# Attention by even and odd heads on partition halves, and a feed-forward in token groups of 512 with output chunks of 128, in a block of windowed attention and Fourier layer

## Chip, cores, metric

One core of a Trainium2 chip. The metric is the device time of one launch in microseconds (us). Most runs of one kernel lie within 0.3% of its median. A ratio compares the fast runs of one kernel with the fast runs of the kernel before in the same rounds, as the record gives it, with a 95% interval. It is not quite the ratio of the medians that stand beside it.

## The reference, cut to what matters

32 images of 56 by 56 tokens and 128 channels, all in fp32.

```python
# layer 0: windows of 7x7 (49 tokens), shifted by 3, 4 heads of 32 channels
q, k, v = split(win @ w_qkv.T)                      # per window and head: 49 x 32
attn = softmax(scale * q @ k.T + bias + mask)       # 49 x 49
x = x + unwindow((attn @ v) @ w_proj.T + b_proj)    # groupnorm of x ahead of it
# layer 1: along rows and along columns: DCT, 32 modes, a 128x128 mix per mode, inverse DCT
h = fourier_rows(gn(x), w0) + fourier_cols(gn(x), w1)
x = x + relu(h @ W1 + b1) @ W2 + b2                 # 128 -> 512 -> 128, 3136 tokens an image
```

## The kernel before

A "row" is one row of eight windows; an image has eight, so there are 256. Each engine works through its own queue of instructions in the order of the built program. The build may shift independent pieces against each other. An edit of the source's order therefore sets the built order only indirectly. Attention of one image is issued row by row; the Fourier layer and feed-forward of the image before (`conv_layer`) is a generator. Each of its pieces ends with a `yield` of its estimated TensorE time, and the main loop lets it run a share ahead of the next row's scores and a share ahead of this row's output:

```python
    for R, (b, i) in enumerate(rows):
        im = images[b]
        share = PE_CONV / NWR / 2 if R >= NWR + LAG else 0.0
        # ... loading and norm of the next image (cut)
        advance(share)                       # run conv_layer pieces for `share` us
        if R + 1 < len(rows):
            attn_scores(images[rows[R + 1][0]], rows[R + 1][1])
        advance(share)
        attn_out(im, i)
```

The weighted values: four transposes of the softmax (TensorE), a copy out of PSUM, the memory that TensorE writes, into `aT` (VectorE; such a copy is called an evacuation below), then the product with a `v` whose second half holds zeros, so that the result comes out per pair of heads:

```python
            for m in range(4):
                nc.tensor.transpose(pt[:, m * P : (m + 1) * P], a[:, hp, pr]..., ident)   # cut
            aT = work.tile([P, 4, 2, JP], F32, tag="aT", name="aT")
            nc.vector.tensor_copy(aT.rearrange("p m a j -> p (m a j)"), pt)
            ...
                        nc.tensor.matmul(
                            po3[hp * JP : (hp + 1) * JP, :, x0 : x0 + s1 - s0],
                            lhsT=v[:, w, hp].rearrange("j h d -> j (h d)"),
                            rhs=aT[:, 2 * (w4 // 2) + hp, w % 2, 0:WT]...,              # cut
                            start=True, stop=True)
```

The inverse transform of rows and the feed-forward. `back` makes two transposes (TensorE), one copy into `zT` (ScalarE) and eight products (TensorE); `rows_back` then adds the result to `xf` (VectorE):

```python
        rows_back(0)
        yield 0.65
        for g in range(NG):                  # 7 groups of 448 tokens
            ...
            for f in range(NF):              # first product (FF1): 4 x 448 columns
                nc.tensor.matmul(ph[:, :GT], lhsT=wff1[:, f * P : (f + 1) * P], rhs=xf[group g], ...)
                nc.scalar.activation(hf, ph[:, :GT], AF.Relu, bias=b1sb[:, f : f + 1])
            yield 3.0
            if g + 1 < NG:
                rows_back(g + 1)             # one group ahead, BETWEEN the two products
                yield 0.65
            for c in range(4):               # second product (FF2): 4 chunks of 112 tokens
                for f in range(NF):
                    nc.tensor.matmul(pf[:TC, ...], lhsT=hid[f][:, c * TC : (c + 1) * TC], rhs=wff2[:, f], ...)
            ...
            yield 3.5
```

Of the kernel before, what the change touches and what calls it, by code (L numbers as in the profile page):

```python
# [15 lines left out]
P = 128  # L16
S = 56
# [24 lines left out]
HIDBUFS = 5  # L42
LAG = 1
# [4 lines left out]
def swin_fourier_kernel(  # L48
# [104 lines left out]
    mask_sb = const_load([P, 2, 3, WT], shift_mask.rearrange("r s p j -> p r s j"), "mask")  # L153
    bm = const.tile([P, 2, 2, NWR // 2, 2, WT], F32, tag="bm", name="bm")
    rpb_f = rpb.rearrange("p (t h) y x -> p t h (y x)", t=2)
    for r in range(2):
        for pr in range(NWR // 2):
            for t in range(2):
                nc.vector.tensor_tensor(
                    bm[:, r, t, pr],  # L160
                    rpb_f[:, t],
                    mask_sb[:, r, 0 if pr < NWR // 2 - 1 else 2]
                    .unsqueeze(1)
                    .to_broadcast([P, 2, WT]),
                    ALU.add,
                )
# [21 lines left out]
    b2sb = const_load([TC, C], b2.partition_broadcast(TC), "b2sb")  # L188
# [9 lines left out]
    q_sb, v_bd, a_sb = [], [], []  # L198
    for i in range(2):
        q_sb.append(big.tile([P, RT + JP - WT], F32, tag=f"q{i}", name=f"q{i}"))  # L200
        v_bd.append(big.tile([P, NWR, 2, 2, HD], F32, tag=f"v{i}", name=f"v{i}"))
        a_sb.append(big.tile([P, 2, NWR // 2, 2, JP], F32, tag=f"a{i}", name=f"a{i}"))
        nc.gpsimd.memset(q_sb[i], 0.0)
        nc.gpsimd.memset(v_bd[i], 0.0)
        nc.gpsimd.memset(a_sb[i], 0.0)
# [7 lines left out]
    def image_begin(b):  # L213
        im = Image()
        im.b = b
        im.x = xls.pop(b) if b in xls else load_image(b)
        im.xw = big.tile([P, NWR, RT], F32, tag="xw", name="xw", bufs=2)
        im.st = small.tile([P, NWR, 6], F32, tag="st0", name="st0", bufs=2)
        im.part = small.tile([TC, 2, C // 4, NWR], F32, tag="part", name="part", bufs=2)
        im.scr = dram.tile([S, S, C], F32, tag="scr", name="scr", bufs=2)  # L220
        return im

    def image_group(im, i):



        pt = attn_bank()
        pt4 = pt[:, : 8 * S].rearrange("p (j r s) -> p j r s", r=8, s=WS)
        for c in range(4):
            nc.tensor.transpose(  # L230
                pt4[:, :, 2 * c : 2 * c + 2],
                im.x[:, WS * i // 2 + c],
                ident_x[:, :, SS:].rearrange("p r (j s) -> p j r s", s=WS),
            )
        mine = pt4[:, :, i % 2 : i % 2 + WS].rearrange("p j r s -> p j (r s)")
        xw = im.xw[:, i]
        nc.scalar.copy(xw.rearrange("p (j t) -> p j t", t=WT), mine)
        nc.vector.bn_stats(im.st[:, i], xw)

        n0, n1 = WS * i // 2, WS * (i + 1) // 2  # L240
        piece = im.x[:, n0:n1]
        nc.gpsimd.tensor_tensor(  # L242
            piece, piece, bproj.unsqueeze(1).to_broadcast([TC, n1 - n0, C]), ALU.add
        )
# [36 lines left out]
    def attn_scores(im, i):  # L281

        q, v, a = q_sb[i % 2], v_bd[i % 2], a_sb[i % 2]
        src = im.xw[:, i]
# [16 lines left out]
        wv = im.w[:, 2 * C : 3 * C].rearrange("c (p h d) -> c h p d", h=2, d=HD)  # L301
        for w in range(NWR):
            for hh in range(2):
                nc.tensor.matmul(  # L304
                    pv[hh * JP : hh * JP + WT, w * JP : (w + 1) * JP],
                    lhsT=src[:, w * WT : (w + 1) * WT],
                    rhs=wv[:, hh],
                    start=True,
                    stop=True,
                )  # L310
        for hh in range(2):
            rows = slice(hh * JP, hh * JP + WT)
            nc.scalar.copy(  # L313
                v[rows, :, :, hh].rearrange("j w p d -> j (w p) d"),
                pv[rows].rearrange("j (x d) -> j x d", d=HD),
            )


        ps = [attn_bank(), attn_bank()]
        for w in range(NWR):  # L320
            for hp in range(2):
                cs = slice(hp * JP, (hp + 1) * JP)
                qs = slice((w % 2) * JP, (w % 2 + 1) * JP)
                nc.tensor.matmul(  # L324
                    ps[hp][qs, (w // 2) * 2 * WT : (w // 2 + 1) * 2 * WT],
                    lhsT=q[cs, w * WT : w * WT + JP],
                    rhs=k_bd[cs, w].rearrange("c h j -> c (h j)"),
                    start=True,
                    stop=True,
                )  # L330
        NR = NWR // 2 * 2
# [3 lines left out]
        for hp in range(2):  # L335
            a3 = a[:, hp].rearrange("p a h j -> p (a h) j")[:, :, 0:WT]
            nc.vector.tensor_tensor(  # L337
                a3,
                ps[hp][:, :RT].rearrange("p (m j) -> p m j", j=WT),
                bm[:, i // (NWR - 1), hp].rearrange("p a h j -> p (a h) j"),  # L340
                ALU.add,
            )
        a3 = a.rearrange("p t a h j -> p (t a h) j")[:, :, 0:WT]
# [12 lines left out]
    def attn_out(im, i):  # L356

        v, a = v_bd[i % 2], a_sb[i % 2]
        po = attn_bank()
        po3 = po[:, :RT].rearrange("p (r x) -> p r x", x=S)  # L360
        for hf in range(2):
            pt = attn_bank()
            for m in range(4):
                pr, hp = 2 * hf + m // 2, m % 2
                nc.tensor.transpose(  # L365
                    pt[:, m * P : (m + 1) * P],
                    a[:, hp, pr].rearrange("p h j -> p (h j)"),
                    ident,
                )
            aT = work.tile([P, 4, 2, JP], F32, tag="aT", name="aT")  # L370
            nc.vector.tensor_copy(aT.rearrange("p m a j -> p (m a j)"), pt)  # L371
            for w4 in range(4):
                w = 4 * hf + w4

                x0 = w * WS + SS
                cuts = ((0, WS, x0),) if w < NWR - 1 else ((0, WS - SS, x0), (WS - SS, WS, 0))
                for s0, s1, x0 in cuts:
                    for hp in range(2):
                        nc.tensor.matmul(  # L379
                            po3[hp * JP : (hp + 1) * JP, :, x0 : x0 + s1 - s0],  # L380
                            lhsT=v[:, w, hp].rearrange("j h d -> j (h d)"),
                            rhs=aT[:, 2 * (w4 // 2) + hp, w % 2, 0:WT].rearrange(
                                "j (r s) -> j r s", s=WS
                            )[:, :, s0:s1],
                            start=True,
                            stop=True,
                        )

        if i % 2 == 0:
            im.oT = work.tile([P, 2 * RT], F32, tag="oT", name="oT")  # L390
        oT = im.oT
        nc.scalar.activation(
            oT[:, i % 2 * RT : (i % 2 + 1) * RT], po[:, :RT], AF.Identity, bias=im.bias[:, 2:3]
        )
# [35 lines left out]
    def conv_layer(im):  # L430
# [158 lines left out]
        rows_back(0)  # L589
        yield 0.65  # L590
        for g in range(NG):
            res = work.tile([TC, 4, C], F32, tag="res", name="res")
            nc.sync.dma_start(
                res, im.scr[8 * g : 8 * g + 8].rearrange("(n r) w c -> (r w) n c", r=2)
            )
            nc.gpsimd.tensor_tensor(  # L596
                res, res, b2sb.unsqueeze(1).to_broadcast([TC, 4, C]), ALU.add
            )
            hid = []
            for f in range(NF):  # L600
                ph = conv_bank()
                nc.tensor.matmul(  # L602
                    ph[:, :GT],
                    lhsT=wff1[:, f * P : (f + 1) * P],
                    rhs=xf[:, 8 * g : 8 * g + 8].rearrange("p r w -> p (r w)"),
# [3 lines left out]
                hf = work.tile([P, GT], F32, tag="hid", name="hid", bufs=HIDBUFS)  # L609
                nc.scalar.activation(hf, ph[:, :GT], AF.Relu, bias=b1sb[:, f : f + 1])  # L610
                hid.append(hf)
            yield 3.0
            if g + 1 < NG:
                rows_back(g + 1)
                yield 0.65
            pf = conv_bank()
            for c in range(4):
                for f in range(NF):
                    nc.tensor.matmul(  # L619
                        pf[:TC, c * C : (c + 1) * C],  # L620
                        lhsT=hid[f][:, c * TC : (c + 1) * TC],
                        rhs=wff2[:, f],
                        start=(f == 0),
                        stop=(f == NF - 1),
                    )
            nc.vector.tensor_tensor(
                res, pf[:TC].rearrange("p (n c) -> p n c", c=C), res, ALU.add
            )
            for n0, n1, p, dst in chunks_of(out, b, 4 * g, 4 * g + 4):
                nc.sync.dma_start(dst, res[p, n0 - 4 * g : n1 - 4 * g])  # L630
            yield 3.5
# [106 lines left out]
```

## Time and profile before

| | before |
|---|---|
| median of the first three runs | 4977.4 us (4976.43 to 4993.0) |
| span of the profiled run | 4980.0 us, granted clock 0.977 |
| TensorE busy, and idle (span less busy) | 4641.3, 338.7 us |
| ScalarE, VectorE busy | 2491.8, 2428.6 us |
| TensorE passes; changes of the array's tiling | 64320; 3342 |

The granted clock is the mean share of TensorE's full clock in the trace. A tiling is the size of the parts into which TensorE's array is split for a matmul (64 by 32: 64 rows, 32 columns). An fp32 matmul shows as two passes. "Perfetto Trace Analysis" in the Trainium skill, in the note ahead of its first section, calls matmul busy time a bad metric because matmuls are pipelined; the trace agrees: one experiment below runs the very same 64320 passes and is busy 4689.8 us instead of 4641.3. To separate work from waiting I also counted over the starts in the trace: the *waits* are what lies between two successive starts beyond the usual step of the form (as given in the prediction), 93 ns for a change of tiling and the longer first step after one; what is left of the span is the *work*. By this count the kernel before has 4470 us of work and 510 of waits. The count is good to some tens of us: a second count, with slightly different steps, gave 54 to 80 us more waits for every kernel told of here, but the same differences to the kernel before within 22 us.

The lines of a piece of work differ between the kernels. For reading the profiles below:

| piece | engine | before | after |
|---|---|---|---|
| scores | TensorE | L324 | L330 |
| subtract of the maximum, exp, sum | GpSimd, ScalarE, VectorE | L346, L349, L350 | L352, L355, L356 |
| transposes of the softmax, copy to `aT`, weighted values | TensorE, VectorE, TensorE | L365, L371, L379 | L373, L379, L385 |
| projection | TensorE | L400 | L420 |
| transposes of z, copy to `zT`, inverse transform, add to `xf` | TensorE, ScalarE, TensorE, VectorE | L544, L550, L555, L582 | L564, L570, L575, L602 |
| FF1, FF2 | TensorE | L602, L619 | L642, L656 |

### The profile page before, as it was taken

What the parts mean: (1) busy time and instruction counts of PE and PEld (TensorE: products, weight loads), DVE (VectorE), ACT (ScalarE), POOL (GpSimd) and SP (SyncE); (2) the same over time, 40 slices, a digit from 0 to 9 for tenths busy, and PEclk for the clock granted to TensorE, in tenths of its full rate; (3) what the DMA queues carried; (4) which work ended last, traced back from release to release, by engine and by line L of the source; (5) the groups of instructions that cost most, each with busy time, mean ns of one, the idle gap of its engine ahead of it and who ended that gap; (6) DMA issues with size and microseconds to landing.
All of it is one profiled execution on the core that took longest, in us unless ns stands there. A gap on an engine that the chain in (4) does not pass through costs nothing.

```text
span 4980.0 us, 143896 instructions
## 1 busy us (share of the span) xinstructions
PE 4641.3 (93%) x64320; PEld 3587.0 (72%) x64320; DVE 2428.6 (49%) x4469; ACT 2491.8 (50%) x4705; POOL 1385.5 (28%) x1071
## 2 busy tenths in 40 slices
PE   4799999999999999999999999999999999999998
PEld 3677777777777777777777777777777777777776
DVE  3554445554554545445544455544455544555441
ACT  2445555555555455554555555455554555554553
POOL 2222222232222323222232222222223232222220
PEclk8799999999999999999999999999999999999999
DMA  3111222212222212222212222122222122222111
GB/s 79 39 51 43 60 58 57 65 45 49 58 58 59 65 38 52 60 58 59 58 38 60 57 56 65 45 49 57 57 61 64 41 50 60 58 61 60 35 46 51
DMA packets 533292, 271.74 MB, mean 55 GB/s; under 512 B 29360, under 2 KB 532289, under 8 KB 532417
## 3 DMA queue, kind: packets, MB, share of 16 engines
q1 hardware_dynamic: 521272, 257.03, 20.3%
q8 instruction: 504, 8.26, 0.7%
q10 hardware_dynamic: 11400, 5.51, 0.4%
q14 instruction: 116, 0.94, 0.1%
HBM read 159.66 MB, written 102.76 MB: 53 GB/s over the span
## 4 chain that ended last, share of the span: by engine, by line
PE 72%; DVE 10%; ACT 7%; POOL 5%; issue 3%; DMA 2%; ACTq 1%; SPq 0%; POOLq 0%; DVEq 0%
PE pc L619 14%; PE pc L602 11%; PE pa L324 6%; PE pa L379 6%; PE pc L526 5%; PE pa L304 5%; POOL a L346 5%; PE pa L400 5%; PE pc L555 5%; PE pa L286 4%; PE pa L291 3%; DVE mx L345 3%; PE pa L365 2%; ACT a L349 2%; PE pa L230 2%
## 5 line engine op out<-in xcount | busy, mean ns | idle before, releaser
L619 PE MATMUL pc<-wff,hid 128*112 128x128 f32 x7168 | 926.5, 283 | 0.7 <-ACT hid L610 0.6
L619 PEld LDWEIGHTS pc<-wff,hid 128*112 128x112 f32 x7168 | 840.8, 182 | 55.1 <-issue 14.6
L346 POOL TENSOR_TENSOR a<-a,mx 128x784 f32<-128x784 f32 x256 | 389.0, 1519 | 1700.2 <-DVE mx L345 1586.2
L610 ACT ACTIVATE hid<-pc,b1sb 128x448 f32<-128x448 f32 x896 | 568.3, 634 | 487.4 <-PE pc L602 446.9
L602 PE MATMUL pc<-xf,wff 128*128 128x448 f32 x1792 | 781.1, 553 | 0.8 <-DVE xf L582 0.8
L349 ACT ACTIVATE a<-a 128x784 f32<-128x784 f32 x256 | 223.5, 873 | 835.5 <-POOL a L346 835.5
L297 DVE TENSOR_SCALAR k_bd<-pa,bqkv 32x392 f32<-32x392 f32 x512 | 320.7, 626 | 619.8 <-ACT k_bd L299 613.7
L352 POOL TENSOR_TENSOR a<-a,rs 128x784 f32<-128x784 f32 x256 | 389.1, 1520 | 678.1 <-DVE rs L351 595.8
L596 POOL TENSOR_TENSOR res<-res,b2sb 112x512 f32<-112x512 f32 x224 | 284.8, 1271 | 859.2 <-DMA res<-scr 837.5
L337 DVE TENSOR_TENSOR a<-pa,bm 128x392 f32<-128x392 f32 x512 | 284.8, 567 | 408.2 <-PE pa L324 403.5
L379 PEld LDWEIGHTS pa<-aT,v 128*64 128x64 f32 x9216 | 328.9, 142 | 166.4 <-DVE aT L371 121.1
L371 DVE COPY aT<-pa 128x512 f32<-128x512 f32 x512 | 346.1, 676 | 200.2 <-PE pa L365 199.9
L408 DVE TENSOR_TENSOR xl<-pa,xl 112x384 f32<-112x384 f32 (+1 forms) x256 | 159.9, 625 | 579.6 <-PE pa L400 579.6
L350 DVE TENSOR_REDUCE sm<-a 128x16 f32<-128x784 f32 x256 | 248.3, 970 | 387.5 <-ACT a L349 387.5
L324 PE MATMUL pa<-k_bd,q 64*64 64x98 f32 x8192 | 420.8, 252 | 16.6 <-DVE k_bd L297 13.7
L324 PEld LDWEIGHTS pa<-k_bd,q 64*64 64x64 f32 x8192 | 327.4, 133 | 143.4 <-DVE k_bd L297 85.3
L379 PE MATMUL pa<-aT,v 128*64 128x49 f32 (+2 forms) x9216 | 386.8, 227 | 35.7 <-DVE aT L371 33.5
L602 PEld LDWEIGHTS pc<-xf,wff 128*128 128x128 f32 x1792 | 300.4, 190 | 164.5 <-issue 91.8
L304 PEld LDWEIGHTS pa<-wn,xw 128*49 128x49 f32 x8192 | 258.8, 125 | 161.6 <-issue 63.4
L242 POOL TENSOR_TENSOR xl<-xl,bproj 112x384 f32<-112x384 f32 (+1 forms) x256 | 285.2, 1136 | 237.8 <-PE pa L230 234.3
L365 PE MATMUL pa<-ident,a 128*128 128x128 f32 x2048 | 334.8, 287 | 1.1 <-POOL a L352 1.1
L313 ACT COPY v<-pa 49x512 f32<-49x512 f32 x512 | 293.3, 573 | 78.0 <-PE pa L304 72.4
(83 smaller groups left out, 6687.3 us busy)
## 6 DMA issues: line engine op xcount, KB each, us to landing
res<-scr SPq DMA_DIRECT2D x224, 224.0 KB
htok<-scr SPq DMA_DIRECT2D x256, 196.0 KB
out_dram<-res SPq DMA_DIRECT2D x192, 224.0 KB
scr<-xl SPq DMA_DIRECT2D x128, 224.0 KB
xl<-in_x_dram SPq DMA_DIRECT2D x32, 784.0 KB
xl<-in_x_dram SPq DMA_DIRECT2D x32, 672.0 KB
scr<-xl SPq DMA_DIRECT2D x128, 168.0 KB
out_dram<-res SPq DMA_DIRECT2D x32, 112.0 KB
```

The source lines that it names most:

```text
L297: nc.vector.tensor_scalar(dst, pk3[hs], im.bias[hs, 1:2], None, ALU.add)
L304: nc.tensor.matmul(pv[hh * JP : hh * JP + WT, w * JP : (w + 1) * JP], lhsT=src[:, w * WT : (w + 1) * WT], rhs=wv[:, hh], start=True, stop= ...
L324: nc.tensor.matmul(ps[hp][qs, (w // 2) * 2 * WT : (w // 2 + 1) * 2 * WT], lhsT=q[cs, w * WT : w * WT + JP], rhs=k_bd[cs, w].rearrange("c h ...
L346: nc.gpsimd.tensor_tensor(a3, a3, mx2.unsqueeze(2).to_broadcast([P, 2 * NR, WT]), ALU.subtract)
L349: nc.scalar.activation(a3, a3, AF.Exp)
L352: nc.gpsimd.tensor_tensor(a3, a3, rs2.unsqueeze(2).to_broadcast([P, 2 * NR, WT]), ALU.mult)
L365: nc.tensor.transpose(pt[:, m * P : (m + 1) * P], a[:, hp, pr].rearrange("p h j -> p (h j)"), ident,)
L371: nc.vector.tensor_copy(aT.rearrange("p m a j -> p (m a j)"), pt)
L379: nc.tensor.matmul(po3[hp * JP : (hp + 1) * JP, :, x0 : x0 + s1 - s0], lhsT=v[:, w, hp].rearrange("j h d -> j (h d)"), rhs=aT[:, 2 * (w4 / ...
L602: nc.tensor.matmul(ph[:, :GT], lhsT=wff1[:, f * P : (f + 1) * P], rhs=xf[:, 8 * g : 8 * g + 8].rearrange("p r w -> p (r w)"), start=True, ...
L610: nc.scalar.activation(hf, ph[:, :GT], AF.Relu, bias=b1sb[:, f : f + 1])
L619: nc.tensor.matmul(pf[:TC, c * C : (c + 1) * C], lhsT=hid[f][:, c * TC : (c + 1) * TC], rhs=wff2[:, f], start=(f == 0), stop=(f == NF - 1),)
```

## The change

Intent: no product with zeros in the weighted values, fewer and larger evacuations on ScalarE, and fewer, fuller passes in FF2 (25 chunks an image instead of 28). Core of the diff, shortened (constants, masks, residual loads and stores are cut):

```diff
+FF_GROUPS = (HB,) * 5 + (320, 256)
 # values: windows alternate between the partition halves, all 128 channels at once
+            nc.tensor.matmul(pv[w % 2 * JP : (w % 2 + 1) * JP, (w // 2) * C : (w // 2 + 1) * C],
+                lhsT=im.xw[:, t0 : t0 + JP], rhs=im.w[:, 2 * C : 3 * C], start=True, stop=True)
+        nc.scalar.copy(v.rearrange("j p c -> j (p c)"), pv)
 # scores: one matmul of 98 columns for two heads becomes two of 49, even and odd heads on a partition half each
-                    ps[hp][qs, (w // 2) * 2 * WT : (w // 2 + 1) * 2 * WT],
-                    lhsT=q[cs, w * WT : w * WT + JP],
-                    rhs=k_bd[cs, w].rearrange("c h j -> c (h j)"),
+                for u in range(2):
+                        ps[hp][u * JP : (u + 1) * JP, w * WT : (w + 1) * WT],
+                        lhsT=q[cs, w * WT : w * WT + JP],
+                        rhs=k_bd[cs, w, u],
 # weighted values: per head, 49 rows by 32 columns, even and odd windows in a bank each
+                for h in range(NH):
+                    for u in range(2):
+                        ks = slice(u * JP, u * JP + WT)
+                            po[u][h * HD : (h + 1) * HD, pr * WT : (pr + 1) * WT],
+                            lhsT=v[ks, pr, h * HD : (h + 1) * HD],
+                            rhs=aT[ks, 2 * p2 + h // 2, h % 2, 0:WT],
 # output: evacuated by ScalarE (even windows) and by three VectorE instructions (odd ones)
 # feed-forward
-        rows_back(0)
-        yield 0.65
-        for g in range(NG):
+        for n in FF_GROUPS:
+            while back_done * GT < t0 + n:
+                rows_back(back_done)
+                back_done += 1
+                yield 0.65
             ... FF1 on n tokens ...
-            yield 3.0
-            if g + 1 < NG:
-                rows_back(g + 1)
-                yield 0.65
+            yield 3.0 * n / GT
             ... FF2 in chunks of 128 ...
-            yield 3.5
+            yield 3.5 * n / GT
```

One part does not show in the intent: `rows_back`, which stood between the two products and one group ahead, now stands just ahead of the FF1 that reads what it makes.

## The prediction

> **What bounds the kernel now.** I read four views in this order: the page, the groups by form of TensorE, the timeline of TensorE in one stretch of steady work, and the waits. First the page:
>
> ```profile
> span 4980.0 us, 143896 instructions
> PE 4641.3 (93%) x64320; PEld 3587.0 (72%) x64320; DVE 2428.6 (49%) x4469; ACT 2491.8 (50%) x4705; POOL 1385.5 (28%) x1071
> ...
> PE 72%; DVE 10%; ACT 7%; POOL 5%; issue 3%; DMA 2%; ACTq 1%; SPq 0%; POOLq 0%; DVEq 0%
> ```
>
> TensorE is busy 93% and holds 72% of the chain that ends last; VectorE and ScalarE are half idle. The kernel runs attention of one image beside the Fourier part and the feed-forward of the image before, so TensorE nearly always has other work while one of the two waits. What TensorE has to do sets the time, and the change must be read as a change of TensorE work. Now the groups of TensorE that the change touches:
>
> ```profile
> L619 PE MATMUL pc<-wff,hid 128*112 128x128 f32 x7168 | 926.5, 283 | 0.7 <-ACT hid L610 0.6
> L602 PE MATMUL pc<-xf,wff 128*128 128x448 f32 x1792 | 781.1, 553 | 0.8 <-DVE xf L582 0.8
> L324 PE MATMUL pa<-k_bd,q 64*64 64x98 f32 x8192 | 420.8, 252 | 16.6 <-DVE k_bd L297 13.7
> L379 PE MATMUL pa<-aT,v 128*64 128x49 f32 x7168 | 331.0, 230 | 35.7 <-DVE aT L371 33.5 <-issue 0.7
> L304 PE MATMUL pa<-wn,xw 128*49 128x64 f32 x8192 | 310.4, 223 | 0.0
> ```
>
> Each fp32 matmul of the program stands here twice (L324: 32 images, 8 rows, 16 matmuls are 4096, the count is 8192): it runs as two passes. The mean durations overlap, so they can't be summed. The spacing of starts is what counts, and the timeline of TensorE gives it:
>
> ```profile
> 2095.87 2.42 PE L602 MATMUL pc<-xf,wff 128*128 128x448 f32 x6
> 2098.22 0.67 PE L379 MATMUL pa<-aT,v 128*64 128x49 f32 x16
> ...
> 2103.92 3.75 PE L619 MATMUL pc<-wff,hid 128*112 128x128 f32 x32
> ...
> 2108.92 1.10 PE L304 MATMUL pa<-wn,xw 128*49 128x64 f32 x32
> 2109.95 1.02 PE L602 MATMUL pc<-xf,wff 128*128 128x448 f32 x2
> 2110.90 0.89 PE L324 MATMUL pa<-k_bd,q 64*64 64x98 f32 x16
> 2111.72 1.02 PE L602 MATMUL pc<-xf,wff 128*128 128x448 f32 x2
> ```
>
> From these and from the single starts in the trace I take these **steps**. L619 has one pass per 109 ns ((3.75-0.27)/31 is 112, the first being longer). L602 has one per 376 ns. L324 starts passes in pairs, on two column halves of the array, one pair per 84 ns; L379 one pair per 58 ns; L304 one pair per 56 ns. L555 (64 by 64 tiles in all four corners) starts four per 96 ns. Two bounds explain all of them. The moving columns take 0.834 ns each ((376-84)/(448-98)) plus some 2.5 ns: 98 columns make 84, 64 make 56, 448 make 376. But L379 moves 49 columns, which would be 43, and L526 moves 56, which would be 49, and both have 58: there the load of 64 weight columns is the bound.
>
> **A switch of the array's tiling** also costs. Six passes of L602 after a transpose, which has the same tiling, last 2.35 us to the next start: 6 times 376 is 2.26, and 0.09 is left. Two passes between runs of other tilings last 0.95: 0.75 plus 0.20. So leaving a tiling costs 93 ns (the median of all six kinds of switch lies at 90 to 94), and the first step after it 40 to 50 ns more in a tiled mode, 57 to 104 in the full array.
>
> The view of waits shows what TensorE waits for, at most some hundred us of each:
>
> ```profile
> PEld pc L555 <- ACT zT L550: 174.5, 232, 1.8
> PEld pa L379 <- DVE aT L371: 121.1, 213, 1.5
> PEld pa L324 <- DVE k_bd L297: 85.3, 230, 1.6
> ```
>
> **What the Trainium skill says.** "TensorE: Matmul & The Clock Gate", Part 3, The mechanism, says that tiles of the array with different positions run at once, starts about 4 ns apart; here the starts within a pair or four lie 5 to 7 ns apart, so it holds, with a slightly larger gap. The same page, LDWEIGHTS, gives columns/1.2 ns, whatever the rows: 53 ns for 64, 27 for 32 (an estimate from that page); the trace has steps of 58 where the load is the bound, 5 more. "TensorEngine Tiling (Array Packing)", Key Properties, says that a change of the tiling mode drains TensorE; the 93 ns above agree. Its Gotcha 1 says that different row tiles may not write one PSUM bank at once, which is why the change gives the two window parities a bank each; no run shows that yet.
>
> **The change part by part.** Rows of windows: 32 images by 8 are 256.
>
> Scores. Before, a row had 16 matmuls of 98 columns; after, 32 of 49 columns, the same weights (64 columns of q) loaded for both column halves. The built program still issues one half of the partitions first and then the other in 195 rows, so two tiles run at once there, and in 61 rows (62 before) all four. The columns would allow 43 ns a pair, but the load of 64 weight columns allows 58. Before: 194 rows by 16 steps by 84, and 62 rows by 8 steps by 84, are 302 us. After: 195 by 32 by 58.4 and 61 by 16 by 58.4 are 421 us. **+119 us**, and some +11 because 184 rows issue the first of these matmuls alone.
>
> Weighted values. Before, 18 matmuls a row at 64 columns of weights, half of which were zeros: 36 passes in 18 pairs by 58.4 is 1.05 us. After, 32 matmuls of 49 rows by 32 columns in eight tile positions. If all eight run at once, a row takes 8 steps, each bounded by the issue of eight passes at 6.7 ns, 54 ns: 0.44 us, an estimate. **-156 us.** This tiling, 64 by 32, is not in the trace before.
>
> Values. 16 matmuls of 64 columns become 8 of 128: 16 steps of 56 become 8 of 109. **-6 us.**
>
> Feed-forward. The first product keeps its 3136 tokens and 28 matmuls an image: no change. The second has 25 chunks instead of 28, so 100 matmuls instead of 112: 224 passes by 109 become 200 by about 112 (128 weight columns, an estimate). 24.4 us become 22.4. **-65 us** in 32 images.
>
> Switches. Counting changes of tile size in the order of the built programs: 3342 before, 3904 after, because 64 by 32 is a mode of its own and because the last chunk of 64 tokens is one too. 562 times 93 is 52, and the longer first steps add about 21. **+73 us.**
>
> Sum: 119+11-156-6-65+73 is **-24 us** of TensorE work.
>
> Other engines, beside it. ScalarE loses one of two evacuations of the values (573 ns a row, 147 us) and half of the output evacuation (587 to about 350, 61 us). VectorE gains three evacuations a row of 147, 28 and 21 columns, from the rows of L337, L582 and L277 about 350, 220 and 210 ns: 0.78 us, 200 us in all, and goes to 53%. None comes near the bound. But the projection now waits for VectorE's queue too. The program puts at least 0.3 us of other matmuls before it in 248 rows, so I count no loss. Fewer waits for ScalarE (its zT copies cost TensorE some 200 us) and more for VectorE about cancel. I take +10 for the inverse transform of columns, which now stands just ahead of the feed-forward that needs it. 4977-24+10, rounded up for doubt about the eight tiles, gives **4970 us**.
>
> **The rivals.** (1) The eight tiles don't all run at once. With four at a time the weighted values take 16 steps of about 50, 0.8 us a row, and the gain falls from 156 to some 64 us: about 5060. For it: no such tiling was measured here, and the bursts issue instructions faster than anything in this kernel. Against: L555 shows four tiles with a 7 ns gap and no sign of a limit. (2) The load of weights isn't the bound of the scores, or both partition halves overlap as they do in L555; then a row takes 32 by 43 or less, and about 80 to 100 us more are saved: about 4880. Against: L379 and L526 both sit at 58 whatever they move. (3) VectorE's queue becomes a wait: each row ends 0.3 us later on its chain, in part uncovered. 256 times 0.3 is 77 us: about 5045. For it: waits for aT and k_bd, both VectorE's, are already 200 us. Against: TensorE has filler almost everywhere. (4) ScalarE's relief shows: half of the waits for zT go, about 4880.
>
> **Range and chances.** The sum is a small difference of large terms, each known to perhaps a third: 40 us for the scores, 50 for the weighted values, 20 for the feed-forward, 30 for switches, and 50 for waits. Together some 90. I take 4880 to 5060. Within 2% means 4878 to 5077; both ends need a rival to be right alone. Faster 0.15, same 0.76, slower 0.09; more weight below, since rivals 2 and 4 could add up.
>
> **What would show it.** The scores' passes in pairs per 58 ns; the weighted values in groups of eight per 54 ns, so a run of 32 passes in some 0.4 us; the second feed-forward product at 6400 passes with 111 ns each; busy ScalarE near 2290 and VectorE near 2620; the count of passes up from 64320 to about 75000. The prediction is wrong if the score pairs come at 43 ns, if the weighted values come in fours or twos, or if waits for oT, zT or aT ahead of TensorE move by over 60 us in sum.

(What the prediction calls "the inverse transform of columns" in its sum is this `rows_back`, which works along rows.)

## More of the kernel before

TensorE's busy time is a sum over modelled ends, so I use it for idle time only.

## Result, and the profile after

Slower: 5214.44 us median of 4 runs (5212.44 to 5230.66), against 4980.56 of the 4 runs before in the same rounds. The ratio is 1.0472 (1.0444 to 1.0501). The predicted 4970 and its range of 4880 to 5060 are both missed. The page of the kernel after:

```profile
span 5213.4 us, 165986 instructions
PE 4674.0 (90%) x74816; PEld 3546.2 (68%) x74816; DVE 2590.7 (50%) x5270; ACT 2303.2 (44%) x4449; POOL 1367.5 (26%) x1134
```

The time is 233 us longer, and TensorE's idle time went from 338.7 to 539.4. By my count over starts, its work went from 4470 to 4460, as good as unchanged, and its waits from 510 to 753: +243. The loss is waiting. (The view of the chain that ended last is of no help here: it breaks off in this run and shows 0%.)

The groups by form of TensorE show where. Columns: busy, mean ns of one, then idle time just before and what ended it. Kernel before, three groups:

```profile
L400 PE MATMUL pa<-wproj,oT 128*112 128x128 f32 x1792 | 262.3, 288 | 22.0 <-ACT oT L392 19.9
...
L555 PE MATMUL pc<-idctw,zT 64*64 64x112 f32 x3584 | 193.4, 272 | 79.3 <-ACT zT L550 76.8
...
L555 PE MATMUL pc<-idcth,zT 64*64 64x112 f32 x3584 | 141.6, 275 | 45.4 <-ACT zT L550 42.4
```

Kernel after, the same view:

```profile
L330 PE MATMUL pa<-k_bd,q 64*64 64x49 f32 x16384 | 583.7, 221 | 2.4 <-DVE k_bd L306 1.4 <-ACT k_bd L308 0.2
...
L420 PE MATMUL pa<-wproj,oT 128*112 128x128 f32 x1792 | 262.7, 289 | 91.4 <-DVE oT L412 34.8 <-ACT oT L414 30.2 <-ACT hid L650 26.3
L385 PE MATMUL pa<-aT,v 49*32 49x49 f32 x16384 | 237.2, 219 | 71.3 <-DVE aT L379 63.6 <-issue 7.7
...
L575 PE MATMUL pc<-idctw,zT 64*64 64x112 f32 x3584 | 161.4, 270 | 136.5 <-ACT zT L570 136.5
...
L575 PE MATMUL pc<-idcth,zT 64*64 64x112 f32 x3584 | 147.1, 283 | 68.0 <-ACT zT L570 64.9
```

The idle time ahead of the inverse transform rose from 119 to 201 us (76.8+42.4 to 136.5+64.9), of the weighted values for `aT` from the 33.5 that the prediction shows to 63.6, and of the projection from 22.0 to 91.4. Counted over starts (by the second count), the waits of TensorE grew by 83 us ahead of the inverse transform, 29 ahead of the weighted values, 61 ahead of FF1 (which waits for `xf`) and 66 ahead of the projection, nearly all of the growth.

The clock is a rival: the trace shows it at half for 229 us of the kernel before and for 331 us of the kernel after. But of the growth of the waits only 34 us lie in such stretches, and e3 below is 2.3% slower at a higher granted clock (0.982) than before.

The timeline of the kernel after shows one of these places. Columns: start us, duration us, engine, line, operation, count, and in brackets the idle time before it and what ended it:

```profile
2036.84 2.94 PE L656 MATMUL pc<-wff,hid 128*128 128x128 f32 x24
...
2039.62 0.60 PE L373 MATMUL pa<-ident,a 128*128 128x128 f32 x4
...
2040.05 0.38 PE L564 MATMUL pc<-ident,z 128*128 128x128 f32 x2
2040.21 0.87 ACT L355 ACTIVATE a<-a 128x784 f32<-128x784 f32 x1 [5.71 <-POOL a L352]
...
2041.11 0.37 ACT L570 COPY zT<-pc 128x256 f32<-128x256 f32 x1
2041.12 0.97 DVE L356 TENSOR_REDUCE sm<-a 128x16 f32<-128x784 f32 x1 [0.55 <-ACT a L355]
...
2041.53 0.61 PE L575 MATMUL pc<-idctw,zT 64*64 64x112 f32 x16 [1.10 <-ACT zT L570]
2042.00 0.68 DVE L379 COPY aT<-pa 128x512 f32<-128x512 f32 x1
...
2042.74 0.41 PE L385 MATMUL pa<-aT,v 49*32 49x49 f32 x32 [0.59 <-DVE aT L379]
...
2043.86 1.92 PE L642 MATMUL pc<-xf,wff 128*128 128x512 f32 x2
```

Read it downwards. FF2 (L656) is over at about 2039.7. TensorE then transposes softmax (L373) and z (L564) and is done at 2040.43. The copy to `zT` could start then, but ScalarE's queue has the exp L355 ahead of it, which itself waited 5.71 us for GpSimd; so L570 starts at 2041.11, when the exp ends. The input of the copy to `aT` is complete at 2040.22, but VectorE's queue has the sum L356 ahead of it, which waits 0.55 us for the exp and then takes 0.97; so L379 starts at 2042.00. TensorE has nothing ready in its own queue: behind the transposes stand L575 (waits for `zT`), then L385 (waits for `aT`), then FF1 L642, which needs `xf`, which needs L575. "Perfetto Trace Analysis", Tensor Engine Instruction (MATMUL, LD_WEIGHTS), says in its note that ScalarE, VectorE and GpSimd are strict first-in, first-out; the starts here agree: `zT`'s copy starts 0.03 us after the exp ended (2040.21+0.87 to 2041.11), and `aT`'s after the sum (its start is recorded 0.09 us ahead of the sum's recorded end, 2041.12+0.97).

In the kernel before, the same place in an attention row has feed-forward matmuls between the transposes and the product that needs their copy:

```profile
2000.09 3.75 PE L619 MATMUL pc<-wff,hid 128*112 128x128 f32 x32
2003.67 0.60 PE L365 MATMUL pa<-ident,a 128*128 128x128 f32 x4
2004.11 2.42 PE L602 MATMUL pc<-xf,wff 128*128 128x448 f32 x6
2006.71 0.67 PE L379 MATMUL pa<-aT,v 128*64 128x49 f32 x16 [0.18 <-DVE aT L371]
```

Six passes of FF1 (2.42 us) cover the copy, and 0.18 us of waiting is left. FF1 could run there since its `xf` was made a group earlier.

One place proves little, so here is a count over the order of TensorE's passes in five traces:

| | before | after | e5 | e1 | e11 |
|---|---|---|---|---|---|
| row transforms (of 224) whose inverse products follow their own z transposes with nothing between | 39 | 131 | 129 | 67 | 39 |
| copies to `aT` (of 512) with FF1 or FF2 between the transposes and the weighted values | 278 | 156 | 186 | 279 | 280 |

The places without cover are many more in the kernel after, and in e5, whose source differs from the kernel before by the place of `rows_back` alone. As an estimate, 92 more row transforms with a wait of 0.6 to 1.1 us each are 55 to 101 us; the idle time for `zT` rose by 82.

### The profile page after: what moved, and what is told of

The parts are those of the page before. It is cut to its first block, busy times and chain, and to the rows that moved or that the text cites. A ratio compares the mean times of both kernels' runs of the same rounds, so it can differ in the third digit from the quotient of the medians.

```text
span 5213.4 us, 165986 instructions
## 1 busy us (share of the span) xinstructions
PE 4674.0 (90%) x74816; PEld 3546.2 (68%) x74816; DVE 2590.7 (50%) x5270; ACT 2303.2 (44%) x4449; POOL 1367.5 (26%) x1134
## 5 line engine op out<-in xcount | busy, mean ns | idle before, releaser
L656 PE MATMUL pc<-wff,hid 128*128 128x128 f32 x6400 | 877.6, 283 | 14.4 <-ACT hid L650 13.4
L642 PE MATMUL pc<-xf,wff 128*128 128x512 f32 (+2 forms) x1792 | 821.2, 581 | 31.3 <-DVE xf L602 31.3
L656 PEld LDWEIGHTS pc<-wff,hid 128*128 128x128 f32 x6400 | 771.5, 189 | 93.1 <-issue 32.0
L650 ACT ACTIVATE hid<-pc,b1sb 128x512 f32<-128x512 f32 (+2 forms) x896 | 564.7, 633 | 593.9 <-PE pc L642 586.6
L330 PE MATMUL pa<-k_bd,q 64*64 64x49 f32 x16384 | 583.7, 221 | 2.4 <-DVE k_bd L306 1.4
L355 ACT ACTIVATE a<-a 128x784 f32<-128x784 f32 x256 | 223.3, 872 | 789.5 <-POOL a L352 789.5
L642 PEld LDWEIGHTS pc<-xf,wff 128*128 128x128 f32 x1792 | 319.8, 200 | 227.7 <-issue 126.8
L379 DVE COPY aT<-pa 128x512 f32<-128x512 f32 x512 | 351.6, 687 | 216.8 <-PE pa L373 210.0
L356 DVE TENSOR_REDUCE sm<-a 128x16 f32<-128x784 f32 x256 | 247.9, 968 | 238.8 <-ACT a L355 235.9
L373 PE MATMUL pa<-ident,a 128*128 128x128 f32 x2048 | 352.1, 294 | 4.9 <-POOL a L358 2.6
L420 PE MATMUL pa<-wproj,oT 128*112 128x128 f32 x1792 | 262.7, 289 | 91.4 <-DVE oT L412 34.8
L314 PEld LDWEIGHTS pa<-wn,xw 128*64 128x64 f32 x4096 | 230.7, 137 | 160.6 <-PE pa L295 51.9
L633 POOL TENSOR_TENSOR res<-res,b2sb 128x512 f32<-128x512 f32 (+2 forms) x256 | 263.1, 1032 | 280.2 <-DMA res<-scr 277.8
L420 PEld LDWEIGHTS pa<-wproj,oT 128*112 128x112 f32 x1792 | 225.6, 184 | 161.7 <-ACT oT L414 55.3
L308 ACT ACTIVATE k_bd<-pa,bqkv 32x392 f32<-32x392 f32 x512 | 298.6, 583 | 55.8 <-DVE k_bd L306 21.7
```

Source lines behind the costliest of these rows:

```text
L308: nc.scalar.activation(dst, pk3[hs], AF.Identity, bias=im.bias[hs, 1:2])
L330: nc.tensor.matmul(ps[hp][u * JP : (u + 1) * JP, w * WT : (w + 1) * WT], lhsT=q[cs, w * WT : w * WT + JP], rhs=k_bd[cs, w, u], start=True, ...
L373: nc.tensor.transpose(pt[:, m * P : (m + 1) * P], a[:, hp, 2 * pr : 2 * pr + 2].rearrange("p w j -> p (w j)"), ident,)
L420: nc.tensor.matmul(pp[:TC, (n - n0) * C : (n - n0 + 1) * C], lhsT=oT[:, (n - base) * TC : (n - base + 1) * TC], rhs=wproj, start=True, sto ...
L642: nc.tensor.matmul(ph[:, :n], lhsT=wff1[:, f * P : (f + 1) * P], rhs=xff[:, t0 : t0 + n], start=True, stop=True,)
L650: nc.scalar.activation(hf[:, :n], ph[:, :n], AF.Relu, bias=b1sb[:, f : f + 1])
```

## The experiments

The expectations name the theories so. Theory A (placement): the loss comes from `rows_back` standing just ahead of FF1. Theory B (attention): it comes from the new tiles, their switches and evacuations. Theory C, from e5 on: the groups of 512 with their unequal ends make the waits, whatever the place. Theory D, from e5 on: the order of the kernel before was tuned, and any change of order costs. All kernels told of gave correct results. "Waits" are by my count over starts, like the 510 and 753 above. All edits to the order of the program keep every dependence.

**e1: the change, with `rows_back` put back between the products.**

```diff
-        for n in FF_GROUPS:                                     # (lines joined)
-            while back_done * GT < t0 + n:
-                rows_back(back_done); back_done += 1; yield 0.65
+        while back_done * GT < FF_GROUPS[0]:
+            rows_back(back_done); back_done += 1; yield 0.65
+        for gi, n in enumerate(FF_GROUPS):
             ... FF1 ...
             yield 3.0 * n / GT
+            if gi + 1 < len(FF_GROUPS):
+                while back_done * GT < t0 + n + FF_GROUPS[gi + 1]:
+                    rows_back(back_done); back_done += 1; yield 0.65
```

> The changed kernel with one thing put back: the inverse row transform of the next feed-forward group is issued between the first and the second product of the group before, as in the kernel before, and not just ahead of the product that needs it. Theory A (placement): the changed kernel lost its time because transpose, zT copy, inverse transform and first product then stand in TensorE's queue with nothing between; putting it back takes away some 180 us of waits and about 45 us of tiling switches, to about 4990 us. Theory B (attention): the waits come from the short runs of the weighted values and from the output's way over VectorE; then only the switches go, to about 5170 us.

Measured: 5049.83 us, ratio 1.0111 (1.0081 to 1.0141) to the kernel before. Waits 605. About 165 of the 234 us are gone with this move alone (5214.44 less 5049.83, of different rounds). What is left, 1.1%, this edit does not touch.

**e2: the attention of the change, with the feed-forward of before.**

> The attention of the changed kernel with the feed-forward of the kernel before (groups of 448, chunks of 112, the transform between the products). By the step sizes that the trace of after shows, TensorE's own work is some 65 us more than before (scores +119, weighted values -156, values -6, the rest switches of tiling and odd runs). Theory A: about 5040 us. Theory B: 5200 us or more, waits as in the changed kernel.

Measured: 5076.82 us, 1.0165 (1.014 to 1.019). Waits 530, so 20 more than before; the work is about 4540 (5070.0 of the profiled span less 530), 70 more than before. It has 3878 changes of tiling, 536 more than before, nearly all that the whole change adds. So the attention part costs some 70 us of TensorE work, and little waiting, by itself. Theory B explains a third of the loss taken alone, but the feed-forward's gain in work should offset that part in the whole change.

**e3: the attention of before, with the feed-forward of the change, placement included.** (The mask's load took another tile's buffer, to make room.)

> The attention of before with the feed-forward of the changed kernel, its transform just ahead of the first product. (The shift mask lies in another tile's buffer at the start, only to make room.) TensorE's own work is about 45 us less than before. Theory A: about 5130 us, since the waits come with it. Theory B: about 4935 us.

Measured: 5107.33 us, 1.0228 (1.0203 to 1.0253). Waits 643. Waits are 133 more than before. Work is only 9 less, where the chunks of 128 were to save 65; 214 more changes of tiling take some 20 us of that back at 93 ns, and the rest lies in what the count can't resolve.

**e4: e3 with `rows_back` between the products,** the edit of e1.

> As the feed-forward alone, but with the transform of the next group between the two products, so the chunks of 128 tokens without the new placement. TensorE's own work is some 90 us less than before (65 of it by 100 matmuls instead of 112 an image). Both theories: about 4890 us. If it is not faster, the groups of 512 themselves (seven of unequal size, two inverse transforms for the first) cost waits, which neither theory holds.

Measured: 5077.23 us, 1.0161 (1.0132 to 1.019). Expected were 4890. Work fell by 47 (5077.0 less 654 is 4423), yet the waits are 654: with groups of 512 and this attention, putting `rows_back` back did not take them away. Theory A as I had it, that placement ahead of FF1 is all there is, fails here, although the cover is back (37 of 224 and 279 of 512 in the count above; e3 has 131 and 62). The view of waits shows the same copies once more: TensorE's idle time for `zT` is 177.6 us (before 119.2), for `aT` 73.7 (33.5), for `oT` 48.1 (19.9), and for a DMA 61.9 (42.9). Why these copies come late in e4 was not traced.

**e5: the kernel before, with nothing changed but the place of `rows_back`.**

```diff
-        rows_back(0)
-        yield 0.65
         for g in range(NG):
+            rows_back(g)
+            yield 0.65
             ... FF1 ...
             yield 3.0
-            if g + 1 < NG:
-                rows_back(g + 1)
-                yield 0.65
```

> The kernel before with the inverse row transform of each group of 448 just ahead of its first product, nothing else: the same matmuls, another place. Theory A (placement alone makes the waits): some 120 us slower, about 5110 us, as the feed-forward alone was, with waits of the inverse transform for zT. Theory C (the groups of 512 with unequal ends make them, whatever the place): within 30 us of before. Theory D (the order was tuned for before and any change of it costs): slower, too.

Measured: 5213.75 us, 1.0481 (1.0443 to 1.0518). Waits 752. This is the whole loss, with the same instructions as before: the counts of every engine on its page are those of the page before.

```profile
span 5206.3 us, 143770 instructions
PE 4689.8 (90%) x64320; PEld 3584.3 (69%) x64320; DVE 2438.4 (47%) x4469; ACT 2458.2 (47%) x4705; POOL 1386.9 (27%) x1071
```

Its groups by form (lines as before, FF2 is L616) show the idle time where the kernel after has it, ahead of the inverse transform, the weighted values and FF1:

```profile
L602 PE MATMUL pc<-xf,wff 128*128 128x448 f32 x1792 | 830.7, 587 | 49.0 <-DVE xf L582 49.0
...
L379 PE MATMUL pa<-aT,v 128*64 128x49 f32 x7168 | 328.0, 229 | 120.1 <-DVE aT L371 119.8
...
L555 PE MATMUL pc<-idctw,zT 64*64 64x112 f32 x3584 | 184.1, 272 | 135.3 <-ACT zT L550 135.3
```

And its timeline has the same sequence as the kernel after, with the attention of before:

```profile
2090.76 0.87 ACT L349 ACTIVATE a<-a 128x784 f32<-128x784 f32 x1 [3.44 <-POOL a L346]
...
2090.89 0.38 PE L544 MATMUL pc<-ident,z 128*128 128x128 f32 x2
...
2091.65 0.37 ACT L550 COPY zT<-pc 128x256 f32<-128x256 f32 x1
...
2092.08 0.61 PE L555 MATMUL pc<-idctw,zT 64*64 64x112 f32 x16 [0.81 <-ACT zT L550]
2092.55 0.68 DVE L371 COPY aT<-pa 128x512 f32<-128x512 f32 x1
...
2093.28 0.67 PE L379 MATMUL pa<-aT,v 128*64 128x49 f32 x16 [0.59 <-DVE aT L371]
```

The exp is ahead of the copy to `zT`, the copy to `aT` comes late, and TensorE stands idle for 0.81 and 0.59 us. The kernel after had 1.10 and 0.59. The move is shown to be enough for the size of the loss; neither the new tiles nor the chunks are needed for it. The places are not all the same: by the second count e5 waits 93 us more ahead of the weighted values and 19 less ahead of the projection, where the kernel after has +29 and +66. Theory D forecast a loss here, too; e6 and e9, which change the order in other ways, cost 0.6% and 1.7%.

**e6: the kernel before, with larger estimates in the `yield`s** (3.0 and 3.5 become 3.4 and 4.0, and the total 7 x 6.5 becomes 7 x 7.4), which shifts where the pieces fall between the attention rows.

> The kernel before with every instruction the same; only the weights by which its feed-forward steps are dealt out among the attention rows are changed (3.0 and 3.5 become 3.4 and 4.0, their sum in the total with them). Theory D: the time moves by 50 us or more, upward, with TensorE's own work the same within 10 us. Theories A and C: within 30 us of before.

Measured: 5004.81 us, 1.0057 (1.0027 to 1.0088). Waits 534. Theory D's 50 us or more did not come: this shift of the pieces costs some tenths of a per cent.

**e7: the change, with the two transposes and the copy to `zT` of the next group moved ahead, between the products,** and the eight inverse products left just ahead of FF1.

> The changed kernel with the transposes and the zT copy of the inverse row transform issued one group ahead, between the two products of the group before; the transform's matmuls stay just ahead of the first product. Theory A: the waits of the inverse transform for zT go for the row half (about 100 us of the 145 us they rose), to about 5090 us. If the waits move to the next place where transposes are evacuated (aT, oT, xf), above 5150 us.

Measured: 5179.0 us, 1.0407 (1.0371 to 1.0444), the second of the two outcomes expected. Waits 746. The view of waits of TensorE in e7 (us in total, times, longest):

```profile
PE pa L385 <- DVE aT L379: 156.0, 136, 2.0
PE pc L657 <- DVE xf L616: 72.0, 67, 1.7
PE pc L580 <- ACT zT L572: 64.2, 130, 1.2
```

The wait for `zT` fell from 201 to 64, but the one for `aT` rose from 63.6 to 156, and FF1 (L657) waits 72 for `xf`. Taking away the one wait that the profile names first gained 0.6 points. So the copy to `zT` as such is not the cause. That it is the whole sequence from z to FF1, which has no independent work in it, is my reading; it fits e5 and e1, and e7 does not show it alone. (The 145 us in the expectation leave out that TensorE no longer waits some 66 us for `zT` behind the scores; in sum these waits rose by some 83.)

**e8: the kernel before, with a cheaper form of the intended attention.** The scores stay as before; the weighted values go per head in 64-by-32 tiles, four at once, both row halves into *one* bank (channels in the order of heads 0, 2, 1, 3), and the values are evacuated in one copy.

```diff
-                            po3[hp * JP : (hp + 1) * JP, :, x0 : x0 + s1 - s0],
-                            lhsT=v[:, w, hp].rearrange("j h d -> j (h d)"),
+                        for hh in range(2):
+                            ks = slice(hh * JP, hh * JP + WT)
+                            o = (2 * hh + hp) * HD
+                                po3[o : o + HD, :, x0 : x0 + s1 - s0],
+                                lhsT=v[ks, w, hp],
```

> The kernel before with one part of the change in another form: scores and softmax as before, weighted values in 64 by 32 tiles without zero blocks, one head at a time with the even heads on one half of the partitions and the odd on the other (channels in the order of heads 0, 2, 1, 3, weights permuted to match), four tiles at once, one bank. By the measured steps: weighted values 16 steps of at most 43 ns a row instead of 18 of 58, some -80 us; values 16 steps of 58 instead of 56, +10 us; some 340 switches more, about +45 us. TensorE's own work is some 40 us less. If waits stay: about 4940 us. If theory D holds, they do not stay, and it is 5000 us or more.

Measured: 4987.33 us, 1.0028 (0.9994 to 1.0062): the same. Waits 521 and work 4461, so only some 9 us of work were saved; it has 3678 changes of tiling against 3342, some 31 us at 93 ns, which eat most of what the smaller tiles save.

**e9: the kernel before, with the whole share of a row ahead of the next scores,** none ahead of the output.

```diff
-        advance(share)
+        advance(2 * share)
         if R + 1 < len(rows):
             attn_scores(images[rows[R + 1][0]], rows[R + 1][1])
-        advance(share)
         attn_out(im, i)
```

> The kernel before with every instruction the same; only the feed-forward and Fourier work that is dealt out to each attention row stands wholly ahead of the scores of the next row, where before half of it stood behind them. A control for the next two runs. TensorE's own work is the same within 10 us by its steps and switches. If the time follows the work alone (theory of the prediction): within 30 us of before. Theory D (the order alone moves the waits, and before's order was tuned for before): 40 us or more slower, about 5050 us.

Measured: 5064.65 us, 1.0168 (1.014 to 1.0195). Waits 607. The same instructions in another order again, 1.7% slower.

**e10: e4 with the edit of e9.**

> Attention of before, feed-forward in groups of 512 and chunks of 128 with the transform between the products (as the run of 5077 us), and the dealing out of the control: all of a row's share ahead of the scores. TensorE's own work is about 100 us less than before by steps and switches. Theory D: the 144 us of waits that this feed-forward had gained go with another order, and the saving shows: about 4870 us, faster than before and than the run of 5077 by 200 us. Theory C (groups of 512 cost waits in themselves): it stays at 5000 us or more.

Measured: 4911.33 us, 0.9862 (0.9833 to 0.989). Waits 512, work 4394, which is 76 less than before. Here the saving of the FF2 chunks shows. The edit that cost the kernel before 1.7% took 3 points off e4, so orders can't be judged apart from the kernel that they are in.

**e11: the changed kernel, with order-only edits: that of e1 and that of e9.**

> The changed kernel, attention and all, with two changes of order alone: the transform between the products, and all of a row's share ahead of the scores. TensorE's own work by steps and switches is some 70 us less than before, 95 us less than in the changed kernel. Theory D: about 4920 us, so the changed kernel's loss is all order. If the attention of the change costs in itself more than its steps show (theory B): 5000 us or more.

Measured: 4934.9 us, 0.9905 (0.9882 to 0.9927). Waits 547, so 206 less than in the kernel after. Its page shows the same counts of instructions on all engines as the kernel after, and 401 us of TensorE idle time in place of 539:

```profile
span 4939.7 us, 165871 instructions
PE 4538.4 (92%) x74816; PEld 3447.7 (70%) x74816; DVE 2543.3 (51%) x5270; ACT 2262.2 (46%) x4449; POOL 1365.8 (28%) x1134
```

In its groups by form, the inverse transform waits less than half as long as in the kernel after, while the projection now waits more:

```profile
L420 PE MATMUL pa<-wproj,oT 128*112 128x128 f32 x1792 | 265.7, 290 | 148.2 <-DVE oT L412 87.2 <-ACT zT L570 40.8 <-ACT y L506 18.9
...
L575 PE MATMUL pc<-idctw,zT 64*64 64x112 f32 x3584 | 151.4, 270 | 58.0 <-ACT zT L570 58.0
```

So the changed kernel is not slow for what it computes. In another order the same instructions beat the kernel before by 1%, with 1 outside the interval.

**e12: the attention of e8, the feed-forward of e4, and shares of 1.2 and 0.8 in place of 1 and 1.**

> The candidate to beat both: scores of before, weighted values by single heads in 64 by 32 tiles (the mix that ran in 4987 us), feed-forward of 512 and 128 with the transform between the products, and 0.6 of a row's share ahead of the scores, 0.4 behind. TensorE's own work is some 130 us less than before. Theory D, waits as in before: about 4850 us. If the order is again a bad one, near 4980 us.

Measured: 4885.74 us, 0.9805 (0.9783 to 0.9827). Waits 516. This is the fastest of all, some 330 us faster than the change and about 2% faster than before. It changes several things at once; what each is worth was not separated.

| kernel | ratio to before | waits, us | work, us |
|---|---|---|---|
| before | 1 | 510 | 4470 |
| after | 1.0472 | 753 | 4460 |
| e5: before, `rows_back` moved | 1.0481 | 752 | 4454 |
| e7: after, transposes ahead | 1.0407 | 746 | 4437 |
| e3: FF of the change | 1.0228 | 643 | 4461 |
| e9: before, one share | 1.0168 | 607 | 4459 |
| e2: attention of the change | 1.0165 | 530 | 4540 |
| e4: e3, `rows_back` between | 1.0161 | 654 | 4423 |
| e1: after, `rows_back` between | 1.0111 | 605 | 4444 |
| e6: before, other estimates | 1.0057 | 534 | 4466 |
| e8: cheaper attention | 1.0028 | 521 | 4461 |
| e11: e1 with one share | 0.9905 | 547 | 4393 |
| e10: e4 with one share | 0.9862 | 512 | 4394 |
| e12: e8 and e4, shares 1.2 and 0.8 | 0.9805 | 516 | 4374 |

Work spans 170 us over all kernels, waits 243. e11 and the kernel after have the same instructions, yet the count gives them 4393 and 4460 us of work; 150 fewer changes of tiling explain some 14 us at 93 ns (some more with first steps), and the rest is left open.

## Why the prediction was wrong

Its steps for the work of TensorE held:

- **Scores:** passes in pairs per 58 ns, as predicted; 16384 passes, and a run of 30 to 32 takes 1059 ns.
- **Weighted values:** a run of 32 passes takes 335 ns up to the next start, the switch included; the eight tiles do run at once. Rival 1 falls.
- **Rival 2** falls with the scores' 58 ns.
- **FF2:** 6400 passes at 112 ns, as predicted.
- **Other engines and counts:** ScalarE 2303 (2290 predicted), VectorE 2591 (2620), passes 74816 (75000), changes of tiling 3904, each still 90 to 94 ns.
- **The sum:** -24 us predicted, about -10 by count. e2 puts the attention part at +70 where the prediction's terms (scores, weighted values, values, switches) give about +40; for FF2, e10 has 76 us less work than before and e4 47, against -65 (e3, with its extra changes of tiling, only 9).

The step that failed is the term of waits: "I take +10 for the inverse transform of columns, which now stands just ahead of the feed-forward that needs it." It measured some 165 us in the changed kernel (what e1 takes back) and 239 in the kernel before (e5, 5213.75 less the 4975.05 of its rounds). The term was taken, not worked out. The ground under it was the remark in rival 3 that "TensorE has filler almost everywhere". That was true of the kernel before *because* of where `rows_back` stood: FF1 of a group was ready long before, and it or FF2 covered the copies. The change takes much of this cover away (278 to 156 of 512 copies to `aT`) by making FF1 depend on what is just being made, with FF2 already over. The prediction read the filler as a property of the kernel, when it was a property of the order.

Rival 3 was right in direction for one part: the projection's idle time rose by 69 us in the groups, with VectorE's `oT` 34.8 of it. So the prediction's "I count no loss" there failed as well. It was not the main cause, as e1, with the new evacuations, is back at +1.1%, and e5, without them, has the whole loss. Rival 4 (ScalarE's relief halves the waits for `zT`) was wrong in sign: ScalarE was 8% less busy, and the waits for `zT` grew. Here they hung on what stood ahead of the copy in the queue, not on how full the engine was. (The prediction's "some 200 us" for these waits, and for those of `aT` and `k_bd`, are those of the weight loads, which overlap matmuls; TensorE's matmuls stood idle for 119.2 us for `zT`, 33.5 for `aT` and 13.7 for `k_bd`.)

The prediction's own sign of failure did occur: waits for `zT`, `aT` and `oT` ahead of TensorE moved by about 82, 30 and 45 us, where 60 in sum was set as the limit.

Shown: in the kernel before, the move of `rows_back` is enough for a loss of this size (e5), and undoing it in the changed kernel takes back most (e1). What the move costs depends on the rest of the order: 4.8 points in the kernel before, 3.6 in the changed one, but 0.7 between e3 and e4. Shown too: order alone, with the same instructions, moves the time between -5% (e11 over after) and +4.8% (e5 over before). Not settled: why groups of 512 keep 144 us more waits than before in e4, with `rows_back` placed as before. e10 shows that they are a matter of order as well: its idle time for `zT` is 70.7 us and for `aT` 34.1, against 177.6 and 73.7 in e4. The parts don't add up either: e2 and e3 alone give +1.65% and +2.28%, together less than the change's 4.72%, while e5 alone gives it all.

## What to carry to other kernels

A sum of work gives a floor; with in-order queues, each chain of transpose, copy and matmul needs ready, independent matmuls behind the transpose in TensorE's own queue, and a move of a piece can take these away without adding one instruction. When a diff moves a piece next to its consumer, list in the built order what stands between producer and consumer on every engine, and price the gap as the copy's wait (here 0.6 to 1.1 us each time) times the number of times. If a rewrite that cuts work is slower, run its order change alone on the old kernel first: here one such run (e5) had the whole loss, and two order-only edits made the same rewrite faster than the old kernel.

## What the Trainium skill lacked or had wrong

- "TensorEngine Tiling (Array Packing)", Key Properties, says that a change of mode drains TensorE, but gives no cost: here it is 90 to 94 ns for each of six kinds of change, and the first step after it is 40 to 104 ns longer. The attention part adds 536 of them, about 50 us at 93 ns.
- The same page, Gotcha 1, says that different row tiles can't access one PSUM bank at the same time: in e8 and e12 tiles of both row halves wrote one bank, in different 32-partition blocks, with starts 6 to 7 ns apart, and the results were correct. The limit as worded is too wide.
- "TensorE: Matmul & The Clock Gate", LDWEIGHTS, gives columns/1.2 ns, 53 ns for 64 columns: steps that the load bounds take 58.4 ns here. That it is the load is read from e8: with 32 weight columns and the same 49 moving ones, most steps of four tiles take 43 to 44 ns.
- The same page, Part 3, The mechanism, has starts about 4 ns apart for tiles that run at once: here most starts lie 6 to 7 ns apart. With eight tiles of 64 by 32, 32 passes start within some 201 ns, 6.5 ns each; whether this spacing is the bound there was not tested.
- "Perfetto Trace Analysis" has strict queues and dependency chains, but no page tells what their order alone can be worth: here 4.8% at equal instructions (e5), through copies of 0.4 and 0.7 us that stand behind an exp and a sum.
